# Recurrence steps that add onto Wx written ahead into PSUM, two batches at a time; a last attention tile in two halves; residual adds and stores in order of completion

## The chip, the cores and the metric

The kernel runs on one core of a Trainium2 chip. The metric is the device time of one execution in microseconds (us), the median of several runs. Engines are named as in the profile: PE is TensorE's matrix unit, DVE is VectorE, ACT is ScalarE, POOL is GpSimd, SP is the queue of SyncE that issues transfers.

## The reference

The input is x with 4 batches, 128 channels and 64 x 64 positions, so 4096 tokens a batch; all arithmetic is fp32. Layer 0 is full attention over the positions. Layer 1 works on tokens: causal attention, and then a part called ffn that ends in a recurrence over the 4096 tokens, each with a residual add.

```python
x = x + _L0_conv_ref(_gn(x), ...)           # softmax(q k) v over all positions
t = _to_tokens(x)
t = t + _L1_attn_ref(_ln_t(t), Wq, Wk, Wv)  # causal
t = t + _L1_ffn_ref(_ln_t(t), W, V, gamma, beta)

def _L1_ffn_ref(x, W, V, gamma, beta):
    Wx = x @ W.T                            # then batch norm over all 4 x 4096 tokens
    Wx = (Wx - mean) * rsqrt(var + eps) * gamma + beta
    def step(yt, wx_t):
        yt = sigmoid(wx_t + yt @ V.T)
        return (yt, yt)                     # scanned over the 4096 tokens from y = 0
```

The batch norm needs the statistics of Wx over every token of every batch, so no recurrence step can start before the last attention tile of the last batch is through.

## The kernel before

**Attention.** Batches are taken one after another, layer 0 and then layer 1. A query tile is 512 tokens (QT), eight tiles (NQ) to a batch. A tile is worked off in units of two key blocks of 128: `score` (L855) makes the scores in PSUM (L870 in layer 1, L874 in layer 0), ACT turns them into exponentials (L880, L876), DVE adds them into `total` for the softmax's denominator (L904, L908), and `product` (L889) multiplies by the values into `av` (L911). In layer 1 tile c has 2(c + 1) units, so tile 0 is the shortest and tile 7 the longest; the last four key blocks of each are triangular and are masked on POOL (L883). fp32 matmuls go through PE twice, so the profile counts two for each.

**After a tile.** `finish` (L754 to L787) turns `total` into the reciprocal of the denominator by a chain of small DVE operations (t, tt, part, side, z, rb), scales `av` into o (L775), multiplies by the value weights (po, L781) and adds the residual (L786). In layer 1, `ffn` (L730 to L752) then takes the layer norm's statistics (`deviations`, L679: PE transposes pt_f, bn_stats, POOL's power at L557), spreads them (`spread`, L694), multiplies by W (pw, L744) into w (L746), copies w into WX (ACT, L748) and takes bn_stats of it for the batch norm (L751). These pieces are generators; after each unit one piece of the tile just ended and one of the front of a list are run (`step`, L924), so their instructions stand between the units of the next tile, and PE meets them in this order.

WX of a batch is [128 channels, 32, 128]: token s * 32 + l is at [l, s]. The tokens are thus cut into 128 chunks of 32, and the recurrence runs on all chunks at once.

**Recurrence.** After the last w, DVE forms the batch norm's gain and bias (fmv, L958; fgain and fbias to L964). A chunk's true start value is not known, so 12 warm-up steps over the end of the chunk before it come first (WARM), from 0.5, and then 32 steps. Each of the 44 steps has one `advance` for each of the four batches: a matmul py = V y (L973), z = Wx * gain + py on DVE (L975), and the sigmoid with the bias on ACT (L976), which writes y over WX or, during the warm-up, over `first`:

```python
nc.tensor.matmul(ps[:, :n], lhsT=FV, rhs=y, start=True, stop=True)
nc.vector.scalar_tensor_tensor(z[:, :n], w, gain, ps[:, :n], ALU.mult, ALU.add)
nc.scalar.activation(dst, z[:, :n], AF.Sigmoid, bias=bias)
```

**End.** After each fourth step the four finished steps of every batch are added to the attention's result (L992; Y holds batches 0 to 2, X the last): 30 adds on POOL, and the last one of batches 1 and 3 on DVE. The batches are stored in the order 1, 0, 3, 2 (L996), one half issued from SP and one from ACT. A test follows of whether warm-up and true values agree (ok, good, wrong: L1002 to L1017); the engines read its result and branch, to a slower general kernel if it fails.

Of the kernel before, what the change touches and what calls it, by code (L numbers as in the profile page):

```python
# [30 lines left out]
P = 128  # L31
# [437 lines left out]
SAME = 2.0e-6  # L469


@with_exitstack
def fast_kernel(
# [78 lines left out]
    WX = {}  # L552
# [6 lines left out]
    with ExitStack() as actx:  # L559
# [13 lines left out]
        gn, K0, QR, V0, V1, Q, R1 = {}, {}, {}, {}, {}, {}, {}  # L573
# [10 lines left out]
        def merge1():  # L584
# [8 lines left out]
            wt = tmp.tile([P, 3, P], F32, tag="a", name="wt")  # L593
            center(wt, pw[:, : 3 * P].rearrange("p (a c) -> p a c", a=3), 3)
            yield
            pm = misc("pm1")
            nc.tensor.matmul(pm[:, :P], lhsT=wt[:, 0, :], rhs=wt[:, 1, :], start=True, stop=True)
# [3 lines left out]
            nc.tensor.transpose(pf[:, :P], wt[:, 2, :], ident)  # L601
# [29 lines left out]
        def keys0(b, c):  # L631

            if c == 0:
                K0[b] = kv.tile([P, N], F32R, tag="K0", name=f"K0_{b}")
                QR[b] = kv.tile([P, N // 2], F32, tag="QR", name=f"QR_{b}")
                V0[b] = wxpool.tile([P, NB, C], F32, tag="V0", name=f"V0_{b}")
# [42 lines left out]
        def deviations(src, eps, name):  # L679

            pt = misc(f"pt_{name}")
            for j in range(4):
                nc.tensor.transpose(pt[:, ts(j, P)], src[:, ts(j, P)], ident)  # L683
            stats = small.tile([P, 4, 6], F32, tag="lst", name=f"lst_{name}")
            mv = small.tile([P, 4, 2], F32, tag="lmv", name=f"lmv_{name}")
            for j in range(4):
                nc.vector.bn_stats(stats[:, j, :], pt[:, ts(j, P)])  # L687
            for j in range(4):
                nc.vector.bn_aggr(mv[:, j, :], stats[:, j, :])
            rstd = small.tile([P, 4], F32, tag="rstd", name=f"rstd_{name}")  # L690
            rsqrt(rstd, mv[:, :, 1], eps, 4)
            return pt, mv, rstd

        def spread(r, name):  # L694

            g = small.tile([P, 4, 4], F32, tag="g", name=f"g_{name}")
            for q in range(4):
                nc.vector.tensor_copy(g[0:32, :, q], r[ds(32 * q, 32), :])
            for q in range(1, 4):
                nc.vector.tensor_copy(g[ds(32 * q, 32), :, :], g[0:32, :, :])  # L700
            rb = tmp.tile([P, QT], F32, tag="r", name=f"rb_{name}", bufs=2)
            nc.vector.transpose(
                rb.rearrange("p (k j) -> p k j", j=32),
                g.rearrange("p j q -> p (j q)").unsqueeze(2).to_broadcast([P, 16, 32]),
# [25 lines left out]
        def ffn(b, c):  # L730
            if c == 0:
                last = b == B - 1
                WX[b] = wxpool.tile(
                    [P, CHUNK, NC], F32, tag="V0" if last else f"WX{b}", name=f"WX_{b}"
                )
            src = X2[b][:, ts(c, QT)]
            if b < len(kept):
                nc.sync.dma_start(out=kept[b][:, ts(c, QT)], in_=src)
            yield
            _, _, rstd = deviations(src, 1e-5, f"f_{b}_{c}")  # L740
            yield
            rb = spread(rstd, f"f_{b}_{c}")
            pw = misc(f"pw_{b}_{c}")
            nc.tensor.matmul(pw, lhsT=FWc, rhs=src, start=True, stop=True)  # L744
            w = tmp.tile([P, QT], F32, tag="w", name=f"w_{b}_{c}")
            nc.vector.tensor_tensor(w, pw, rb, ALU.mult)  # L746
            n = QT // CHUNK
            nc.scalar.copy(  # L748
                WX[b][:, :, ts(c, n)].rearrange("p l s -> p s l"), w.rearrange("p (s l) -> p s l", l=CHUNK)
            )  # L750
            nc.vector.bn_stats(stats_f[:, b * NQ + c, :], w)  # L751
            yield  # L752

        def finish(b, layer, c, av, total):  # L754

            name = f"{layer}_{b}_{c}"
            t = tmp.tile([P, QT], F32, tag="a", name=f"t_{name}")
            nc.vector.tensor_tensor(t, total[:, 0, :], total[:, 1, :], ALU.add)  # L758
            tt = tmp.tile([P, QT], F32, tag="b", name=f"tt_{name}")
            nc.vector.transpose(tt, t)  # L760
            part = small.tile([P, 16], F32, tag="part", name=f"part_{name}")
            nc.vector.tensor_reduce(part, tt.rearrange("p (k j) -> p k j", j=32), AX.X, ALU.add)
            yield
            side = small.tile([32, 4, 16], F32, tag="side", name=f"side_{name}")
            for q in range(4):
                nc.vector.tensor_copy(side[:, q, :], part[ds(32 * q, 32), :])
            z = small.tile([P, 16], F32, tag="z", name=f"z_{name}")
            nc.vector.tensor_reduce(z[0:32, :], side.rearrange("j q k -> j k q"), AX.X, ALU.add)
            nc.vector.reciprocal(z[0:32, :], z[0:32, :])
            for q in range(1, 4):  # L770
                nc.vector.tensor_copy(z[ds(32 * q, 32), :], z[0:32, :])
            rb = tmp.tile([P, 16, 32], F32, tag="a", name=f"rb_{name}")
            nc.vector.transpose(rb, z.unsqueeze(2).to_broadcast([P, 16, 32]))  # L773
            o = tmp.tile([P, QT], F32, tag="b", name=f"o_{name}")
            nc.vector.scalar_tensor_tensor(  # L775
                o, rb.rearrange("p k j -> p (k j)"), GUARD, av, ALU.mult, ALU.mult
# [3 lines left out]
            po = misc(f"po_{name}")  # L780
            nc.tensor.matmul(po, lhsT=W1v if layer else W0v, rhs=o, start=True, stop=True)  # L781
            xt = X[b][:, ts(c, QT)]
            if layer and c == 0:
                X2[b] = xpool.tile([P, N], F32, tag="X2", name=f"X2_{b}")
            dst = X2[b][:, ts(c, QT)] if layer else xt
# [4 lines left out]
        units = []  # L790
        for b in range(B):
            for layer in range(2):
                for c in range(NQ):
                    n = 2 * (c + 1) if layer else NP
                    units += [(b, layer, c, u, n) for u in range(n)]
# [11 lines left out]
        def done(key):  # L807
            if key in todo:
                todo.remove(key)
            if key in ends:  # L810
                ends.remove(key)
                _, b, layer, c = key
                if layer == 0:
                    put(("p1", b, c), prepare1(b, c))
                else:
                    put(("f", b, c), ffn(b, c))

        def begin_tile(b, layer, c):

            if layer == 0:  # L820
# [6 lines left out]
                if c == 3 and 0 < b < B - 1:  # L827
                    for k in range(NQ):
                        whole(("f", b - 1, k))
# [8 lines left out]
            else:  # L838
# [5 lines left out]
                if c + 1 < NQ:  # L844
                    todo.insert(0, ("q1", b, c + 1))
                    made["q1", b, c + 1] = after(b, c + 1)

        def after(b, c):
            whole(("e", b, 0, c))
            whole(("p1", b, c))  # L850
# [4 lines left out]
        def score(i):  # L855
            b, layer, c, u, n = units[i]
            if u == 0:
                begin_tile(b, layer, c)
# [208 lines left out]
```

## Time and profile before

| | us |
|---|---|
| median of 3 runs (2596.47 to 2599.96) | 2597.79 |
| the profiled execution | 2599.04 |
| its span in the profile | 2596.9 |
| last exponentials of the attention start (L880) | 2482.61 |
| last w (L746) starts | 2498.78 |
| table load for the sigmoid (L976), 1.28 long | 2502.93 |
| first sigmoid starts | 2504.23 |
| first store issued (L996) | 2571.12 |

The span is what the profile's page covers, from the first to the last event on the core; the execution's own time is 2.1 us longer. A busy share is an average over the span. The clock row gives the clock that PE was granted, in tenths of full speed, in 40 slices. In the chain of waits each line is a start, a length, an engine and a group of instructions, from what ended last back to what released it; in the timeline, a bracket gives the idle time ahead of an instruction and who ended it.

### The profile page before, as it was taken

How to read it: one execution, taken by the hardware profiler on the slowest of the kernel's cores; microseconds unless marked ns; L12 is line 12 of the kernel's file. 1: busy time of each engine (PE TensorE's matmuls, PEld its weight loads, DVE VectorE, ACT ScalarE, POOL GpSimd, SP SyncE). 2: the span in 40 equal slices, each digit the busy share in tenths (PEclk: the TensorE clock that was granted, in tenths of full speed). 3: DMA queues.
4: the chain of work that ended last, by engine and by line, in shares of the span. 5: the costliest groups of instructions: out<-in, count | busy, mean ns of one | idle time of the engine just before them, and what ended most of it. 6: DMA issues, size and time to landing. Idle time of an engine off the chain costs nothing.

```text
span 2596.9 us, 22102 instructions
## 1 busy us (share of the span) xinstructions
PE 2524.0 (97%) x7480; PEld 1358.2 (52%) x7480; DVE 1781.3 (69%) x3631; ACT 1153.5 (44%) x1458; POOL 231.1 (9%) x304
## 2 busy tenths in 40 slices
PE   7999999999999999999999999999999999999975
PEld 4555554444555555444555555444455555544454
DVE  7776667567867667666876666756776766776566
ACT  4444434444444444444444443444444444344455
POOL 2010001111000100110000010111100000000016
PEclk9999999999999999999999999999999999999987
DMA  2000000000100000000100000000010000000013
GB/s 72 1 0 1 0 1 13 9 4 4 37 0 1 0 1 5 12 7 6 37 0 1 1 0 1 12 9 5 5 37 0 1 1 1 0 1 1 0 65 131
DMA packets 11945, 31.31 MB, mean 12 GB/s; under 512 B 2096, under 2 KB 2864, under 8 KB 10032
## 3 DMA queue, kind: packets, MB, share of 16 engines
q1 hardware_dynamic: 8928, 24.12, 2.6%
q10 hardware_dynamic: 2896, 5.71, 0.6%
q8 instruction: 60, 0.98, 0.2%
q14 instruction: 61, 0.50, 0.1%
HBM read 15.14 MB, written 14.68 MB: 11 GB/s over the span
## 4 chain that ended last, share of the span: by engine, by line
PE 90%; DVE 6%; issue 2%; POOL 1%; ACT 1%; DMA 0%; SPq 0%; POOLq 0%; ACTq 0%; DVEq 0%
PE av L911 48%; PE ps L874 17%; PE ps L870 17%; PE py L973 2%; PE po L781 2%; DVE total L904 1%; PE pq L724 1%; PE pk L645 1%; PE pw L744 1%; POOL rstd_f L557 1%; PE pt L683 1%; DVE lst_f L687 0%; PE pt L661 0%; PE pt_f L683 0%; DVE w L746 0%
## 5 line engine op out<-in xcount | busy, mean ns | idle before, releaser
L911 PE MATMUL av<-s,V 128*128 128x512 f32 (+3 forms) x3200 | 1465.9, 580 | 5.1 <-ACT s L876 4.5
L904 DVE TENSOR_TENSOR total<-total,s 128x1024 f32<-128x1024 f32 x676 | 824.5, 1220 | 510.3 <-ACT s L876 309.6
L876 ACT ACTIVATE s<-ps,shift 128x1024 f32<-128x1024 f32 x512 | 569.1, 1114 | 772.7 <-PE ps L874 742.5
L911 PEld LDWEIGHTS av<-s,V 128*128 128x128 f32 x3200 | 594.7, 189 | 543.6 <-issue 477.0
L874 PE MATMUL ps<-q,K 128*128 128x512 f32 x2048 | 759.6, 493 | 2.0 <-DVE K L656 1.4
L880 ACT ACTIVATE s<-ps,zero,R 128x512 f32<-128x512 f32 (+1 forms) x576 | 395.8, 738 | 458.4 <-PE ps L870 457.7
L874 PEld LDWEIGHTS ps<-q,K 128*128 128x128 f32 x2048 | 386.7, 189 | 290.7 <-issue 236.2
L870 PE MATMUL ps<-q,X 128*128 128x512 f32 (+3 forms) x1152 | 500.5, 557 | 0.0
L870 PEld LDWEIGHTS ps<-q,X 128*128 128x128 f32 x1152 | 217.0, 190 | 244.4 <-issue 234.4
L557 POOL TENSOR_TENSOR rstd<-rstd,mhalf 128x4 f32<-128x4 f32 x32 | 32.7, 1023 | 1015.5 <-DVE rstd L556 1015.5
L883 POOL TENSOR_SCALAR_AFFINE_SELECT s<-s 128x128 f32<-128x128 f32 x128 | 46.6, 368 | 506.3 <-ACT s L880 505.8
L908 DVE TENSOR_TENSOR total<-total,s 128x256 f32<-128x256 f32 (+1 forms) x120 | 56.3, 493 | 43.0 <-POOL s L883 42.9
L642 POOL TENSOR_SCALAR X<-X,B0v 128x512 f32<-128x512 f32 x32 | 59.6, 1865 | 243.8 <-DVE xg L640 238.1
L786 DVE SCALAR_TENSOR_TENSOR X<-po,X 128x512 f32<-128x512 f32 x64 | 44.0, 687 | 52.5 <-PE po L781 52.0
L748 ACT COPY WX<-w 128x512 f32<-128x512 f32 x32 | 35.2, 1100 | 96.5 <-DVE w L746 96.5
L557 POOL TENSOR_TENSOR rstd_f<-rstd_f,mhalf 128x4 f32<-128x4 f32 x32 | 35.4, 1108 | 412.2 <-DVE rstd_f L556 412.2
L715 DVE TENSOR_SCALAR V<-pt,lmv,rstd 128x128 f32<-128x128 f32 x128 | 43.8, 405 | 35.8 <-POOL rstd L557 35.8
L975 DVE SCALAR_TENSOR_TENSOR z<-WX,fgain,py 128x128 f32<-128x128 f32 (+1 forms) x176 | 56.4, 347 | 6.2 <-PE py L973 1.8
L675 DVE TENSOR_TENSOR q<-QR,qh 64x512 fp32r<-64x512 f32 x64 | 43.9, 685 | 6.3 <-PE ps L874 5.6
L758 DVE TENSOR_TENSOR t<-total 128x512 f32<-128x512 f32 x64 | 44.3, 692 | 4.5 <-PE pfw L601 2.5
L775 DVE SCALAR_TENSOR_TENSOR o<-rb,av 128x512 f32<-128x512 f32 x64 | 43.8, 684 | 4.4 <-DVE rb L773 0.5
L760 DVE STREAM_TRANSPOSE tt<-t 128x512 f32<-128x512 f32 x64 | 45.4, 709 | 1.8
(120 smaller groups left out, 1328.3 us busy)
## 6 DMA issues: line engine op xcount, KB each, us to landing
X<-in_x SPq DMA_DIRECT2D x28, 256.0 KB, 5.6
kept<-X SPq DMA_DIRECT2D x24, 256.0 KB, 2.0
Y<-kept SPq DMA_DIRECT2D x6, 1024.0 KB, 7.4
out<-Y SPq DMA_DIRECT2D x3, 1024.0 KB, 8.8
out<-Y ACTq DMA_DIRECT2D x3, 1024.0 KB, 9.3
X<-in_x ACTq DMA_DIRECT2D x4, 256.0 KB, 5.7
out<-X SPq DMA_DIRECT2D x1, 1024.0 KB, 14.0
out<-X ACTq DMA_DIRECT2D x1, 1024.0 KB, 14.7
```

Source lines behind the costliest of these rows:

```text
L557: nc.gpsimd.tensor_tensor(dst, dst, mhalf[:, :n], ALU.pow)
L642: nc.gpsimd.tensor_scalar(xt, xt, B0v, None, ALU.add)
L781: nc.tensor.matmul(po, lhsT=W1v if layer else W0v, rhs=o, start=True, stop=True)
L870: nc.tensor.matmul(ps[:, h, first[h] :], lhsT=lhsT, rhs=q[:, first[h] :], start=True, stop=True)
L874: nc.tensor.matmul(ps[:, h, :], lhsT=lhsT, rhs=q[:, k, :], start=k == 0, stop=k == 1)
L876: nc.scalar.activation(s, ps, AF.Exp, bias=shift)
L880: nc.scalar.activation(part, ps[:, h, first[h] :], AF.Exp, scale=scale, bias=zero)
L904: nc.vector.tensor_tensor(total, total, s, ALU.add)
L908: nc.vector.tensor_tensor(t, t, s[:, h, first[h] :], ALU.add)
L911: nc.tensor.matmul(av[:, first[h] :], lhsT=V[:, 2 * u + h, :], rhs=s[:, h, first[h] :], start=u == 0 and h == 0, stop=u == n - 1 and h == 1,)
L973: nc.tensor.matmul(ps[:, :n], lhsT=FV, rhs=y, start=True, stop=True)
L975: nc.vector.scalar_tensor_tensor(z[:, :n], w, gain, ps[:, :n], ALU.mult, ALU.add)
```

## The change

- WX of the batches is held in pairs (WXp), and V0, layer 0's values, is a view of the last one, which the pool's tags gave before.
- In the recurrence the batches go in pairs g = 0 and 1. `seed` writes Wx * gain for four steps of a pair into two banks of PSUM on DVE; two such blocks of each pair are in flight, which takes all eight banks. `advance` adds V y onto it by a matmul without a start flag, and ACT takes the sigmoid from PSUM. Before the first two blocks of each pair, matmuls with zeros (`nil`) are made over the banks. The first block is seeded step by step.
- In layer 1 of the last batch the tiles go 0, 1, 2, 4, 5, 6, 7, 3 (LAST = 3), and the last one in two halves of 256 queries, with 7 and 8 units. `finish`, `ffn`, `deviations` and `spread` take an offset and a width.
- The last product is followed by a sigmoid of one element, so that the table is loaded there.
- POOL adds batches 0, 1 and 2, without batch 2's last two blocks; after the last step DVE adds these, and the whole of batch 3 in two halves. The stores go in the order 0, 1, 2, 3.

```diff
-    WX = {}
+
+    WXp = [wxpool.tile([P, 2, CHUNK, NC], F32, name=f"WX{g}") for g in range(B // 2)]
+    WX = [WXp[b // 2][:, b % 2] for b in range(B)]
...
-                V0[b] = wxpool.tile([P, NB, C], F32, tag="V0", name=f"V0_{b}")
+                V0[b] = WX[B - 1].rearrange("p l s -> p (l s)").rearrange("p (n c) -> p n c", c=C)
...
-        def ffn(b, c):
-            if c == 0:
-                last = b == B - 1
-                WX[b] = wxpool.tile(
-                    [P, CHUNK, NC], F32, tag="V0" if last else f"WX{b}", name=f"WX_{b}"
-                )
-            src = X2[b][:, ts(c, QT)]
+        def ffn(b, c, off, w):
+            name = f"f_{b}_{c}_{off}"
+            cols = ds(c * QT + off, w)
+            src = X2[b][:, cols]
             if b < len(kept):
-                nc.sync.dma_start(out=kept[b][:, ts(c, QT)], in_=src)
-            yield
-            _, _, rstd = deviations(src, 1e-5, f"f_{b}_{c}")
-            yield
-            rb = spread(rstd, f"f_{b}_{c}")
-            pw = misc(f"pw_{b}_{c}")
+                nc.sync.dma_start(out=kept[b][:, cols], in_=src)
+            yield
+            _, _, rstd = deviations(src, 1e-5, name)
+            yield
+            rb = spread(rstd, name)
...
+            if off == 0:
+                wt[b, c] = tmp.tile([P, QT], F32, tag="w", name=f"w_{name}")
+            part = wt[b, c][:, ds(off, w)]
+            nc.vector.tensor_tensor(part, pw, rb, ALU.mult)
             nc.scalar.copy(
-                WX[b][:, :, ts(c, n)].rearrange("p l s -> p s l"), w.rearrange("p (s l) -> p s l", l=CHUNK)
+                WX[b][:, :, ds((c * QT + off) // CHUNK, w // CHUNK)].rearrange("p l s -> p s l"),
+                part.rearrange("p (s l) -> p s l", l=CHUNK),
             )
-            nc.vector.bn_stats(stats_f[:, b * NQ + c, :], w)
...
+            if off + w == QT:
+                nc.vector.bn_stats(stats_f[:, b * NQ + c, :], wt.pop((b, c)))
...
+        def finish(b, layer, c, off, w, av, total):
+
+            name = f"{layer}_{b}_{c}_{off}"
+            k = w // 32
+            t = tmp.tile([P, QT], F32, tag="a", name=f"t_{name}")[:, :w]
+            nc.vector.tensor_tensor(t, total[:, 0, :w], total[:, 1, :w], ALU.add)
...
-        units = []
+
+        units, following = [], {}
         for b in range(B):
             for layer in range(2):
-                for c in range(NQ):
-                    n = 2 * (c + 1) if layer else NP
-                    units += [(b, layer, c, u, n) for u in range(n)]
+                order = list(range(NQ))
+                if (b, layer) == (B - 1, 1):
+                    order.append(order.pop(LAST))
+                following.update({(b, layer, c): d for c, d in zip(order, order[1:])})
+                for c in order:
+                    halves = [(0, QT // 2), (QT // 2, QT // 2)] if (b, layer, c) == (B - 1, 1, order[-1]) else [(0, QT)]
+                    for off, w in halves:
+                        n = (c * QT + off + w) // (2 * P) if layer else NP
+                        units += [(b, layer, c, off, w, u, n) for u in range(n)]
...
+            if i == len(units) - 1:
+
+                nc.scalar.activation(small.tile([P, 1], F32, name="sig"), s[:, 1, w - 1 : w], AF.Sigmoid)
...
-        zp = fctx.enter_context(tc.tile_pool(name="z", bufs=2))
-        ps_y = fctx.enter_context(tc.tile_pool(name="ps_y", bufs=1, space=PSUM))
+        ps_y = fctx.enter_context(tc.tile_pool(name="ps_y", bufs=2, space=PSUM))
...
+        nil = small.tile([P, QT], F32R, name="nil")
+        nc.vector.memset(nil.bitcast(F32), 0.0)
+        first = [small.tile([P, 2, NC], F32, name=f"first{g}") for g in range(B // 2)]
+        for g in range(B // 2):
+            nc.vector.memset(first[g], 0.5)
+        steps = list(range(CHUNK - WARM, CHUNK)) + list(range(CHUNK))
+        nk = len(steps) // BL
+        where = {}
+
+        def seed(g, k):
+            ps = where[g, k] = ps_y.tile([P, BL, 2, NC], F32, tag=f"y{g}", name=f"py{g}_{k}")
+            if k < 2:
+                for j in range(0, BL, 2):
+                    nc.tensor.matmul(
+                        ps[:, j : j + 2].rearrange("p j h s -> p (j h s)"), lhsT=nil[:, :P], rhs=nil,
+                        start=True, stop=True,
+                    )
+            j0, lo = steps[k * BL], int(k * BL < WARM)
+            for js in [slice(j, j + 1) for j in range(BL)] if k == 0 else [slice(0, BL)]:
+                nc.vector.tensor_scalar(
+                    ps[:, js, :, lo:].rearrange("p j h s -> p h j s"),
+                    WXp[g][:, :, j0 + js.start : j0 + js.stop, : NC - lo], gain, None, ALU.mult,
+                )
+
+        def advance(g, k, j):
+            n, lo = k * BL + j, int(k * BL < WARM)
+            dst = first[g][:, :, 1:] if lo else WXp[g][:, :, steps[n], :]
+            y = dst if lo else first[g] if n == WARM else WXp[g][:, :, steps[n] - 1, :]
+            ps = where[g, k][:, j, :, lo:]
+            nc.tensor.matmul(ps, lhsT=FV, rhs=y, start=False, stop=True, skip_group_check=True)
+            nc.scalar.activation(dst, ps, AF.Sigmoid, bias=bias)
+
+        def residual(eng, b, ls, cols=slice(0, NC)):
+            xj = X[b].rearrange("p (s l) -> p l s", l=CHUNK)[:, ls, cols]
+            eng.tensor_tensor(xj, xj, WX[b][:, ls, cols], ALU.add)
+
+        for k in range(2):
+            for g in range(B // 2):
+                seed(g, k)
+        for k in range(nk):
+            for j in range(BL):
+                for g in range(B // 2):
+                    advance(g, k, j)
+            if k == WARM // BL - 1:
+                for g in range(B // 2):
+                    nc.vector.memset(first[g][:, :, 0:1], 0.0)
+            for g in range(B // 2 if k + 2 < nk else 0):
+                seed(g, k + 2)
+            if k * BL >= WARM:
+                ls = slice(steps[k * BL], steps[k * BL] + BL)
+                for b in range(3 if k < nk - 2 else 2):
+                    residual(nc.gpsimd, b, ls)
+        residual(nc.vector, 2, slice(CHUNK - 2 * BL, CHUNK))
+        for h in range(2):
+            residual(nc.vector, 3, slice(0, CHUNK), ts(h, NC // 2))
         for b in range(B):
-            nc.vector.memset(first[b], 0.5)
-
-        def advance(b, y, w, dst, n):
-
-            ps = ps_y.tile([P, NC], F32, tag=f"y{b}", name=f"py{b}")
-            nc.tensor.matmul(ps[:, :n], lhsT=FV, rhs=y, start=True, stop=True)
-            z = zp.tile([P, NC], F32, tag=f"z{b}", name=f"z{b}")
-            nc.vector.scalar_tensor_tensor(z[:, :n], w, gain, ps[:, :n], ALU.mult, ALU.add)
-            nc.scalar.activation(dst, z[:, :n], AF.Sigmoid, bias=bias)
-
-        for j in range(CHUNK - WARM, CHUNK):
-            for b in range(B):
-                advance(b, first[b][:, 1:], WX[b][:, j, : NC - 1], first[b][:, 1:], NC - 1)
-        for b in range(B):
-            nc.vector.memset(first[b][:, 0:1], 0.0)
-        for j in range(CHUNK):
-            for b in range(B):
-                y = WX[b][:, j - 1, :] if j else first[b]
-                advance(b, y, WX[b][:, j, :], WX[b][:, j, :], NC)
-            if j % 4 == 3:
-                for b in range(B):
-                    js = slice(j - 3, j + 1)
-                    xj = X[b].rearrange("p (s l) -> p l s", l=CHUNK)[:, js, :]
-                    eng = nc.vector if j == CHUNK - 1 and b % 2 else nc.gpsimd
-                    eng.tensor_tensor(xj, xj, WX[b][:, js, :], ALU.add)
-        for b in (1, 0, 3, 2):
...
-                ok[:, b, 1:], first[b][:, 1:], WX[b][:, CHUNK - 1, : NC - 1], ALU.subtract
+                ok[:, b, 1:], first[b // 2][:, b % 2, 1:], WX[b][:, CHUNK - 1, : NC - 1], ALU.subtract
```

## The prediction

> **What bounds the kernel now.** I read the page's head first, then the chain that ended last, then the tail of that chain stage by stage in the windows and the timeline.
>
> ```profile
> span 2596.9 us, 22102 instructions
> PE 2524.0 (97%) x7480; PEld 1358.2 (52%) x7480; DVE 1781.3 (69%) x3631; ACT 1153.5 (44%) x1458; POOL 231.1 (9%) x304
> ...
> PEclk9999999999999999999999999999999999999987
> ...
> PE 90%; DVE 6%; issue 2%; POOL 1%; ACT 1%; DMA 0%; SPq 0%; POOLq 0%; ACTq 0%; DVEq 0%
> ```
>
> TensorE fills the attention, some 2480 us; of that only the last tile changes, so everything at stake lies in the last 115 us (4% of the span). The chain's end:
>
> ```profile
> 2490.18 2.07 PE po L781 x2
> ...
> 2504.68 60.01 PE py L973 x344
> 2564.98 8.57 DVE Y L992
> ```
>
> Three pieces are seen: a tail after the last attention tile, the recurrence (60.01 us; 43 steps at 1.395), and residual adds with the stores. In the recurrence the windows show PE, DVE and ACT all near full (columns: stretch, length, PE, PEld, DVE, ACT, POOL busy, clock, DMA share, GB/s):
>
> ```profile
> 2500.00:2510.00 10.00, 5.32 (x25) 5.32 (x26) 6.54 (x22) 7.00 (x16) 0.55 (x1) 0.50 0.00 1
> 2550.00:2560.00 10.00, 10.00 (x60) 8.65 (x59) 9.37 (x31) 9.72 (x31) 10.00 (x7) 1.00 0.00 0
> 2575.00:2580.00 5.00, 0.59 (x2) 0.50 (x2) 2.56 (x8) 0.00 (x0) 0.00 (x0) 0.50 1.02 418
> ```
>
> PE's 10.00 overstates it: 60 records of 0.318 us overlap. The first window shows the recurrence starting at half the clock (about 1.71 us a step until 2510.2, 1.36 after). The third shows stores that move 418 GB/s with nothing else running: the end is store-bound. POOL adds back to back from 2550 on, and a DVE add caught beside it is held until POOL is nearly done:
>
> ```profile
> L975 DVE SCALAR_TENSOR_TENSOR z<-WX,fgain,py 128x128 f32<-128x128 f32 (+1 forms) x176 | 56.4, 347 | 6.2 <-PE py L973 1.8
> ...
> 2564.98 8.57 DVE L992 TENSOR_TENSOR Y<-Y,WX 128x512 f32<-128x512 f32 x1
> 2569.59 2.98 POOL L992 TENSOR_TENSOR Y<-Y,WX 128x512 f32<-128x512 f32 x2
> 2571.12 2.79 SPq L996 DMA_DIRECT2D out<-Y  x2
> 2571.55 0.40 ACT L976 ACTIVATE WX<-z,fbias 128x128 f32<-128x128 f32 x1 [6.50 <-POOL Y L992]
> ```
>
> The last line: the final sigmoid sits behind a store in ACT's queue that waits for POOL.
>
> **What the Trainium skill says.** "PSUM — Partial Sum Buffer", The four PSUM rules: only TensorE sets the bits that tell a matmul without a start flag to add rather than overwrite, so a value written by VectorE is added to only where a matmul has set them before. No run here shows it; it is why eight nil matmuls exist. "GPSIMD Engine Reference", Specifications: POOL shares its SBUF interfaces with VectorE, with contention for operations with two SBUF inputs. The trace agrees: the two-input DVE add took 8.57 us against 1.11 for its like at 2573.99, while z, with one SBUF and one PSUM input, stayed at 0.347 beside a full POOL. "TensorE: Matmul & The Clock Gate", Part 1: the clock halves after an idle window; the trace has 0.50 after 2489.7 and again from 2499.95 to 2510.19.
>
> **The change part by part.** All against the profiled execution (2599.04 us, span 2596.9; the median of the runs is 2597.79, so differences carry over and the level is 1.25 lower).
>
> *Up to batch 3's layer 1* the instruction order per engine is unchanged: 0.
>
> *1. Recurrence.* Before, a batch's chain is ACT 0.402, hand-over 0.05, two fp32 passes 0.21 + 0.275 (spacing, then the last one's record), 0.04, z 0.346, 0.035: 1.36; four z of 0.347 are 1.388. VectorE and the chain bound it equally. Afterwards z is gone and two pairs of 256 columns run. Passes of 256 columns are spaced 0.2135 in the attention; the sigmoid on 256 from PSUM I put at 0.49 ("ScalarE: Activation LUTs", What ACT_TABLE_LOAD costs, gives 280 ns + 0.833 N with a pointer bias, so 493 by estimate; here 396 for 128 against its 387). Chain: 0.05 + (first weights 0.107, two passes 0.427, drain 0.168) + 0.04 + 0.49 = 1.28. PE needs 2 x 0.53 = 1.07 a step, ACT 2 x 0.49 = 0.98: the chain bounds it. 43 x 1.28 + 1.04 (last step of both pairs) = 56.1 against 61.1 (first sigmoid 2504.23 to the regular end 2565.35): **-5.0**. A sigmoid of 0.46 or 0.53 moves this by 43 x 0.035 = 1.5 either way.
>
> The seeds: 128x1024 into PSUM, two per four steps. A DVE pass of 1024 elements takes 1.22 (L904), so 2.44 in a block of 5.12: hidden in DVE, which has nothing else, and each is written a whole block ahead: it waits for the last sigmoid of the block that used its banks and is due one block later. POOL has 3 adds x 1.53 = 4.6 per 5.12: no backlog.
>
> *2. Last tile in two halves.* PE columns stay the same, but half 0's po, transposes and pw now stand before the last score: 0.43 + 0.22 + 0.43 = +1.08. Half 0's po also waits for its o, and here two normalisations meet. From half 0's last score block DVE has, in the built order: t 0.42, tt 0.44, tile 7's four bn_stats 0.95 and aggregates 0.36, part 0.40, rstd 0.17, half 1's copy 0.42, tile 7's g 1.20, rb_f 0.71, w 0.69 and statistics 0.69, side, z and reciprocal 1.65, two totals of half 1 1.38, rb 0.44, o 0.42: 10.3 (256-wide ones scaled from their 512 rows), near 11 with gaps and POOL's rstd between. PE has ten groups of four 256-column passes (pw among them) at 0.85 and 1.1 of smaller ones in that time, 9.6 in all; o reaches PE with the hand-over about 1 to 2 late. Short tiles of batches 0 to 2 show such a hole at 2.1 to 2.3 us (655.3, 1272.0, 1888.8). I take 2.3, bounds 1.5 and 3.5. A clock dip followed one such hole in three, 3.4 us at half speed, 1.7 lost: I take none, bound 1.7. Sum **+3.4** until the last score.
>
> *3. From the last exp to the first sigmoid*, 21.62 us before (2482.61 to 2504.23). Seven DVE passes of 512 become 256 (0.69 to 0.42): -1.9; po cold 2.07 to about 1.0; two bn_stats fewer -0.4; against it half 0's late ffn pieces between them on DVE, +1.3 to 2.2. To the last w: -1.5. Then 8 nil matmuls of 512 stand on PE before the first recurrence matmul, after the last reader of PSUM: 6.8 cold (8 x 0.853), 3.4 warm; the previous stage ends at clock 0.50, so mixed, 6.0, plus 0.75 to the first sigmoid, where before 4.75 passed from w, of which 1.28 was the table load that now hides. 6.75 - 4.75 = +2.0. Together **+0.5** (bounds -2.1, +1.3). The gain chain (fmv 1.03, POOL's pow 0.55) and the short first seeds lie beside the nils. The recurrence then starts warm, which the 5.0 above includes.
>
> *4. End*, R being the end of the last sigmoid. POOL ends batch 0 at R + 1.0 and batch 1 at R + 2.5 (1.53 each); DVE, two inputs, is held until then, then two ok 0.5, batch 2's 1024 elements 2.1 and batch 3's 2 x 4.0 (1.11 for 512 strided, scaled): R + 13.1. Stores start at R + 1.0; 8.39 MB took 23.7 us from first issue to last landing, so R + 24.7 if they don't run dry, and they don't: a batch takes 5 us at 418 GB/s, so batch 2, ready at R + 5, and batch 3 at R + 13 come before the queue is empty at R + 18. Flag: 3.7 us more of DVE and PE to R + 16.8, load and branch 1.5, restart of the engines 7.2 (2579.8 to 2587.0 before), R + 25.5. Final wait to end took 2.0: R + 27 to 27.6 against 31.55 (2565.35 to 2596.9): **-3.95** (bounds -4.5, -1).
>
> Sum: -5.0 + 3.4 + 0.5 - 3.95 = **-5.05**: span 2591.9, and from the median 2597.79 **2592.7 us**. Likeliest case's own range: 2590 to 2596.
>
> **Rivals.**
> A. The half tile gives back the rest: hole 3.5, dip 1.7, nils cold. +1.2 + 1.7 + 0.8: -1.35, **2596.4**. For it: DVE was 0.74 busy already from 2482 to 2492, and gets more. Against: the clock held at two of three such holes.
> B. Slower: the seeds, like the 8.57 us add, are held while POOL adds back to back. Seeds and adds are released by the same sigmoid; held for 4.6, they end 7.0 after the block, where the next but one is due at 5.1: 1.9 lost in each of the six blocks that have both, +11.4: **2604.1**. It decides once a hold exceeds 5.12 - 2.44 = 2.7 us. Against: a seed has one SBUF input, as z has, and z wasn't held.
> C. More gain: hole 1.5 (-0.8), nils nearly warm (-2.5), sigmoid 0.47 (-0.9): -9.25, **2588.5**. For it: PE was fast again between 2496.5 and 2499.95.
> That the sums go wrong through unset bits and the flag sends the work to the general kernel would cost far more; every seeded bank had a nil matmul over its whole width first, so 0.01, inside slower.
>
> **How the numbers follow.** Forecast 0.45, A 0.17, B 0.13, C 0.25. A measurement of this kernel tells 0.2% (5.2 us, 2592.6) from nothing; the forecast lies on that edge: 0.25 faster, 0.20 same. C is faster; A 0.14 same, 0.03 slower with both bounds at the end added; B slower. Faster 0.50, same 0.34, slower 0.16. The range takes in A, C and their bounds, not B: 2585 to 2600.
>
> **What would show it.** Recurrence: sigmoids of one pair 1.28 apart, 43 of them; at 1.36 or more step 1 is wrong. Seeds at 1.2 us: over 3, B. Part 2: the last score 3.4 later, one hole before half 0's po. Part 3: eight nils between the last w and the first sigmoid, 6 us. Part 4: first store 1 us after the last sigmoid, the last landing some 24 later. A landing that waits for DVE's batch 3, or a branch after R + 19, makes the end wrong.

## The result, and the profile after

The changed kernel takes 2594.39 us in the median of 22 runs (2592.44 to 2596.96), the kernel before 2598.97 in as many (2596.24 to 2600.01). The ratio is 0.9985 with an interval of 0.9979 to 0.9992: a gain of about 4 us, clear of the scatter, but smaller than the 0.2% that the prediction took as the least to be told from nothing. The profiled execution has a span of 2592.4 us against 2596.9.

The page of the changed kernel, its head; and from its chain that ended last, the end:

```profile
span 2592.4 us, 21739 instructions
PE 2519.8 (97%) x7372; PEld 1345.1 (52%) x7372; DVE 1760.3 (68%) x3513; ACT 1139.7 (44%) x1386; POOL 219.7 (8%) x297
```

```profile
2506.19 2.33 DVE py L1010 x6
2509.88 3.73 PE py L1020 x8
2566.97 3.34 DVE Y L1025
2570.31 7.68 DVE X L1025 x2
```

Where 60.01 us of PE stood there are only 3.73 in one piece: the chain now changes engine at every step, from matmul to sigmoid and back, so the view leaves the short pieces out. New are the first seeds (L1010) ahead of the recurrence, and DVE's adds behind it.

The timeline of the changed kernel (start, length, engine, line; in brackets the idle time ahead and who ended it) shows the three places that decide, and at its end the verdict of the test:

```profile
2479.69 1.22 PE L788 MATMUL po<-o,W1v 128*128 128x256 f32 x2 [2.58 <-DVE o L782]
...
2502.82 3.75 PE L1004 MATMUL py<-nil 128*128 128x512 f32 x8 [3.35 <-DVE w_f L751]
2503.43 1.02 DVE L981 BATCH_NORM_AGGREGATE fmv<-fstats 128x2 f32<-128x192 f32 x1
...
2506.11 5.14 DVE L1010 TENSOR_SCALAR py<-WX,fgain 128x254 f32<-128x254 f32 x9
...
2508.57 1.12 PE L1020 MATMUL py<-first,FV 128*128 128x254 f32 x4 [2.00 <-DVE py L1010]
2509.36 0.84 ACT L1021 ACTIVATE first<-py,fbias 128x254 f32<-128x254 f32 x2 [6.02 <-PE py L1020]
...
2566.86 3.81 SPq L1049 DMA_DIRECT2D out<-Y  x3
...
2581.33 0.14 DVE L1070 CAST wrong<-good 1x1 int32<-1x1 f32 x1
```

First, PE idles 2.58 us for half 0's o. Second, the matrices of zeros are through at 2506.57, and PE then idles another 2.00 for seeds. Third, the first store goes 1.0 after the last sigmoid ends (2565.87). The windows of the changed kernel (stretch, length, busy time of PE, PEld, DVE, ACT and POOL, clock, DMA share, GB/s) add the clock after the hole, the stores at the end, and what is busy in the middle of the recurrence:

```profile
2479.00:2483.00 4.00, 3.31 (x8) 2.71 (x9) 2.22 (x5) 0.66 (x2) 0.00 (x0) 0.57 0.01 2
...
2575.00:2580.00 5.00, 0.00 (x0) 0.00 (x0) 4.90 (x6) 0.00 (x0) 0.00 (x0) 0.50 1.01 418
```

```profile
2525.00:2545.00 20.00, 18.60 (x65) 9.30 (x64) 9.68 (x9) 15.14 (x32) 14.06 (x10) 1.00 0.01 1
```

The clock fell to half right at the hole. The stores still move 418 GB/s. In the recurrence ACT and DVE stand idle a quarter and half of the time, and PE's 18.60 counts each matmul to its modelled end, while its weight loads are busy 9.30. The timeline of one step:

```profile
2560.87 0.30 PEld L1020 LDWEIGHTS py<-WX,FV 128*128 128x128 f32 x2 [0.49 <-ACT WX L1021]
2561.35 0.30 PEld L1020 LDWEIGHTS py<-WX,FV 128*128 128x128 f32 x2 [0.18 <-ACT WX L1021]
2561.61 0.96 ACT L1021 ACTIVATE WX<-py,fbias 128x256 f32<-128x256 f32 x2 [0.31 <-PE py L1020]
```

In each step of 1.26 PE's weight loads wait 0.67 for ACT, and ACT waits 0.31 for PE. So no engine is full, and a step is bound by one pair's chain.

All kernels below are read by the same five stages, from starts in their timelines: A from the first exponentials of batch 3's layer 1 to the last pair of them; B from there to the last w; C to the first sigmoid; D to the end of the last sigmoid; E to the end of the span.

| kernel | A | B | C | D | E | span |
|---|---|---|---|---|---|---|
| before | 247.20 | 16.17 | 5.44 | 61.12 | 31.55 | 2596.9 |
| changed | 252.75 | 15.37 | 7.11 | 56.51 | 26.53 | 2592.4 |
| e1, tile 7 whole | 247.20 | 17.34 | 7.90 | 55.98 | 26.6 | 2590.2 |
| e9, tile 7 in halves | 251.34 | 13.16 | 7.11 | 56.51 | 26.3 | 2588.3 |
| e2, po later | 249.95 | 15.51 | 7.63 | 55.97 | 26.4 | 2589.1 |
| e3, seeds by bank | 251.26 | 15.36 | 5.11 | 55.29 | 26.4 | 2588.7 |
| e4, no batch 3 add | 252.37 | 15.36 | 7.17 | 56.13 | 21.6 | 2586.8 |
| e8, early batch 3 | 251.27 | 15.36 | 7.63 | 62.92 | 26.4 | 2597.5 |
| e5, end as before | 251.27 | 15.36 | 7.63 | 56.63 | 34.1 | 2601.3 |
| e6, single batches | 251.26 | 15.37 | 5.07 | 47.20 | 28.5 | 2582.9 |
| e7, pairs with z | 251.27 | 15.32 | 4.03 | 80.08 | 26.4 | 2611.8 |
| c2 | 251.27 | 15.36 | 5.07 | 47.08 | 26.9 | 2581.3 |
| c1 | 251.36 | 13.17 | 4.77 | 47.19 | 26.8 | 2578.8 |

(The last sigmoid of before counts at its regular end, 2565.35. e4, e5, e6 and e7 were run once each, the others four times or more.) Three things are to be known for this table.

- Stage A of one and the same code is 251.26 or 251.27 in the six profiles without a clock drop in it (e3, e5, e6, e7, e8, c2), and 252.75 in the changed kernel's, which has one. e4's, 252.37, has a drop too, but is no seventh of these: in its trace tile 7's ffn pieces stand 1.7 us earlier in PE's order.
- The start of stage A, after 2234 us in which PE and ACT do the same instructions in all kernels, scatters from 2233.7 to 2236.4. So 1.3 us of the 4.5 between the two spans (2235.42 before, 2234.12 changed) lie within this scatter and can't be counted for the change.
- Stage C with the changed kernel's seeds is 7.1 where the clock was back at full for the first matmul (changed, e9, e4), and 7.6 where it was still at half with the same last tile (e2, e5, e8).

### The profile page after: what moved, and what is told of

Read it like the earlier page. It is cut to its first block, busy times and chain, and to the rows that moved or that the text cites. A ratio compares the mean times of both kernels' runs of the same rounds, so it can differ in the third digit from the quotient of the medians.

```text
span 2592.4 us, 21739 instructions
## 1 busy us (share of the span) xinstructions
PE 2519.8 (97%) x7372; PEld 1345.1 (52%) x7372; DVE 1760.3 (68%) x3513; ACT 1139.7 (44%) x1386; POOL 219.7 (8%) x297
## 4 chain that ended last, share of the span: by engine, by line
PE 89%; DVE 6%; issue 2%; ACT 1%; POOL 1%; DMA 0%; SPq 0%; POOLq 0%; ACTq 0%; DVEq 0%
PE av L932 48%; PE ps L895 17%; PE ps L888 17%; PE po L788 2%; DVE total L929 1%; PE py L1020 1%; PE pq L730 1%; PE pk L649 1%; POOL rstd_f L561 1%; PE pw_f L747 1%; ACT WX L1021 1%; PE pt L688 1%; DVE lst_f L692 0%; PE pt L665 0%; DVE w_f L751 0%
## 5 line engine op out<-in xcount | busy, mean ns | idle before, releaser
L929 DVE TENSOR_TENSOR total<-total,s 128x1024 f32<-128x1024 f32 (+4 forms) x802 | 881.6, 1103 | 553.4 <-ACT s L897 308.9
L932 PE MATMUL av<-s,WX 128*128 128x512 f32 x2048 | 964.4, 593 | 3.4 <-ACT s L897 3.4
L932 PEld LDWEIGHTS av<-s,WX 128*128 128x128 f32 x2048 | 382.2, 189 | 312.0 <-issue 270.0
L932 PE MATMUL av<-s,V 128*128 128x512 f32 (+3 forms) x1180 | 504.7, 549 | 0.6 <-ACT s L901 0.6
L932 PEld LDWEIGHTS av<-s,V 128*128 128x128 f32 x1180 | 218.8, 191 | 226.1 <-issue 201.6
L794 DVE SCALAR_TENSOR_TENSOR X<-po,X 128x512 f32<-128x512 f32 (+1 forms) x65 | 44.1, 678 | 51.3 <-PE po L788 50.9
L752 ACT COPY WX<-w_f 128x512 f32<-128x512 f32 (+1 forms) x33 | 35.3, 1069 | 93.1 <-DVE w_f L751 93.1
L561 POOL TENSOR_TENSOR rstd_f<-rstd_f,mhalf 128x4 f32<-128x4 f32 (+1 forms) x33 | 36.1, 1094 | 398.6 <-DVE rstd_f L560 398.6
L765 DVE TENSOR_TENSOR t<-total 128x512 f32<-128x512 f32 (+1 forms) x65 | 44.5, 684 | 4.5 <-PE pfw L605 2.5
L782 DVE SCALAR_TENSOR_TENSOR o<-rb,av 128x512 f32<-128x512 f32 (+1 forms) x65 | 43.9, 675 | 4.4 <-DVE rb L780 0.5
```

Of the source, the lines that this page charges most:

```text
L561: nc.gpsimd.tensor_tensor(dst, dst, mhalf[:, :n], ALU.pow)
L765: nc.vector.tensor_tensor(t, total[:, 0, :w], total[:, 1, :w], ALU.add)
L794: nc.vector.scalar_tensor_tensor(dst, po, 1.0 / GUARD, xt, ALU.mult, ALU.add)
L929: nc.vector.tensor_tensor(t, t, s[:, h, f:w], ALU.add)
L932: nc.tensor.matmul(av[:, first[h] : w], lhsT=V[:, 2 * u + h, :], rhs=s[:, h, first[h] : w], start=u == 0 and h == 0, stop=u == n - 1 and h ...
```

## The experiments

### Part 2: the halves

e1 puts the order of the tiles and the last tile back; e9 keeps the halves but cuts tile 7; e2 lets half 0's po stand one unit later.

```diff
# e1 (the first two) and e9 (the first alone)
-LAST = 3
+LAST = 7
-                    halves = [(0, QT // 2), (QT // 2, QT // 2)] if (b, layer, c) == (B - 1, 1, order[-1]) else [(0, QT)]
+                    halves = [(0, QT)]
# e2
+            if w < QT:
+                yield
             po = misc(f"po_{name}")[:, :w]
```

> Tile order of before (tile 7 last) and the last tile whole: part 2 of the change undone, all else as changed. Theory (the halves of tile 3 cost more than they bring): last exponentials start near 2482.6 us as before instead of 2486.9, last w starts 16.2 later (15.4 in the changed kernel), first sigmoid 6.9 after that, so near 2505.9 against 2509.4; recurrence and end as changed; span about 2589, some 3.5 below the changed kernel, 0.997 of before. Rival (the halves pay by the shorter tail, and the matrices of zeros run cold without them): first sigmoid at 2509 or later, span 2592 or more.

> Tile 7 last, in two halves of 15 and 16 units. Theory (the hole at half 0's po comes from tile 7's ffn work meeting half 0's normaliser on DVE, because tile 3 has too few units): with tile 6's ffn done long before, DVE has 5.5 us to do where PE has 9.6, so no hole above 0.5 us and no dip of the clock there; last exponentials near 2483.7, half 0's ffn done before them, last w 13 us later, first sigmoid near 2503.8, span about 2587, 5 below the changed kernel, 0.996 of before. Rival (the hole belongs to halving as such: o follows its half's end too closely): a hole of 2 us or more before half 0's po, last exponentials at 2486 or later, span 2590 or more.

> As changed, with half-width po put one unit later in PE's order. Theory (hole and dip are lost at this place only): hole before half 0's po under 1 us, clock 1.0 in the four us after 2479, last exponentials near 2483.8, about 3 earlier; half 0's ffn ends a unit later, so last w 16 us after them; span about 2590. Rival (DVE is the bound of the whole stretch): the hole returns at a later instruction, last exponentials at 2486 or later, span unchanged at 2592.

Measured: e1 0.9975 of before (0.9964 to 0.9985), first sigmoid at 2507.60; e9 0.9975 (0.9964 to 0.9985), 2505.50; e2 0.9976 (0.9966 to 0.9986), 2506.77. The intervals overlap with that of the change, so the totals alone don't settle it; the stages do. From the start of stage A to the last w, the whole tile 7 takes 247.20 + 17.34 = 264.54, tile 7 in halves 251.34 + 13.16 = 264.50, tile 3 in halves 266.6, with the clock drop 268.1. So cutting tile 7 moves 4 us from behind the last exponentials to ahead of them and gains nothing by itself; with tile 3 it loses 2.1, with the drop 3.6. e1's expectation held in direction, not in size: its tail was 1.2 longer than before's and its stage C a microsecond longer than expected. It gained 2.2 in the span in place of 3.5; its stages are 3.2 shorter in sum, since its stage A began 1.05 later than that of the changed kernel.

The holes, in the timelines of e9 and of e2 (with ACT's copy ahead of it):

```profile
2449.92 0.70 PE L932 MATMUL av<-s,V 128*128 128x256 f32 x2 [1.40 <-ACT s L901]
```

```profile
2476.43 1.06 ACT L752 COPY WX<-w_f 128x512 f32<-128x512 f32 x1 [2.17 <-DVE w_f L751]
...
2477.90 1.15 PE L934 MATMUL av<-s,V 128*128 128x256 f32 x4 [1.24 <-ACT s L903]
...
2479.75 0.59 PE L790 MATMUL po<-o,W1v 128*128 128x256 f32 x2
```

In e9 no wait for o is left, as expected, but a new one of 1.40 stands in the midst of half 0: the theory was right about its hole and missed this one, and the last exponentials came at 2485.2 and not 2483.7. In e2 po starts without a wait and the clock stays at 1.00; a hole of 1.24 is left, for exponentials.

Both holes that are left have one origin, which neither theory had. The copy of the last whole tile's w into WX, on ACT, waits for DVE's w_f and takes 1.06; the next exponentials stand behind it in ACT's queue, and PE's products wait for them. In e9 the copy starts at 2448.46 and the exponentials at 2449.32, in e2 at 2476.43 and 2477.30. In the changed kernel they are as late, at 2476.88 and 2477.75, but there the wait for o covers it.

e2's stage A is 2.8 shorter than that of the profiled changed kernel, near the theory's 3, but 1.5 of this is the clock drop, which six profiles of the same code lack. Against those the edit is worth 1.3. So the theory was right about what it named, and the rival in that a hole came back, though at an earlier instruction than po.

### Part 3: what the first matmul waits for

```diff
-            ps = where[g, k] = ps_y.tile([P, BL, 2, NC], F32, tag=f"y{g}", name=f"py{g}_{k}")
+            ps = where[g, m] = ps_y.tile([P, 2, 2, NC], F32, tag=f"y{g}", name=f"py{g}_{m}")
...
-            for js in [slice(j, j + 1) for j in range(BL)] if k == 0 else [slice(0, BL)]:
-                nc.vector.tensor_scalar(
+            nc.vector.tensor_scalar(
+                ps[:, :, :, lo:].rearrange("p j h s -> p h j s"),
+                WXp[g][:, :, j0 : j0 + 2, : NC - lo], gain, None, ALU.mult,
...
```

> Seeds of two steps, each pair's block in a bank of its own (four in flight), in place of four steps in two banks with the first block step by step. Theory (the first advance waits for all seven single-step seeds ahead of it, 2.7 us, and not for the matrices of zeros): first matmul of the recurrence near 0.8 after the gain is ready and at the end of the zeros, 2506.6 in place of 2508.6; last w to first sigmoid 5.1 in place of 7.1; step unchanged at 1.27; span about 2590.4. Rival (twice the seeds at 0.74 each disturb DVE and the chain, or the zeros are what is waited for): first matmul at 2508 or later, or a step of 1.3 and more, no gain.

Measured: 0.9972 of before (0.9961 to 0.9983). The timeline of e3:

```profile
2502.49 3.75 PE L1003 MATMUL py<-nil 128*128 128x512 f32 x8 [3.34 <-DVE w_f L751]
...
2505.31 0.74 DVE L1007 TENSOR_SCALAR py<-WX,fgain 128x508 f32<-128x508 f32 x1
...
2506.11 6.23 PE L1017 MATMUL py<-first,FV 128*128 128x254 f32 x19
2507.03 1.00 ACT L1018 ACTIVATE first<-py,fbias 128x254 f32<-128x254 f32 x2 [4.02 <-PE py L1017]
```

The recurrence's first matmul starts 0.06 after the first seed's end and follows the zeros with no wait; stage C is 2.0 shorter, as the theory had it. A second gain came with it that was not expected: PE is no longer idle before the recurrence, its clock doesn't drop in the first steps, and stage D is 1.2 shorter. The step itself is unchanged (1.26).

### Part 1: pairs, and z

```diff
# e6: each batch by itself
...
-            ps = where[g, k][:, j, :, lo:]
+            ps = where[b, k][:, j, lo:]
             nc.tensor.matmul(ps, lhsT=FV, rhs=y, start=False, stop=True, skip_group_check=True)
             nc.scalar.activation(dst, ps, AF.Sigmoid, bias=bias)
...
# e7: pairs, z on DVE, no seeds
...
+            nc.tensor.matmul(ps[:, :, lo:], lhsT=FV, rhs=y, start=True, stop=True)
+            nc.vector.scalar_tensor_tensor(
+                z[:, :, lo:], WXp[g][:, :, steps[n], : NC - lo], gain, ps[:, :, lo:], ALU.mult, ALU.add
+            )
+            nc.scalar.activation(dst, z[:, :, lo:], AF.Sigmoid, bias=bias)
...
```

> As changed, with each batch by itself: 176 matmuls and sigmoids on 128 columns, adding onto seeds of 512 elements. Theory (without z the chain of a batch is only 0.98, but then ACT is the bound: four sigmoids of 128 in a step, 0.35 to 0.39 each, and PE's four pairs of passes 1.3): a step of 1.40 to 1.55, recurrence of 61 to 67 us against 56.5. Rival (taking z out was all of it, pairs are no matter): a step of 1.3 or less.

> As changed, in pairs of 256 columns, but with z on DVE as before, no seeds and no matrices of zeros: the fourth of the four cases {pair, single} x {z, seed}, of which the steps so far are single with z 1.36, pair with seed 1.27, single with seed 1.06. Theory (a step is the longer of one group's chain and the busiest engine; a pair makes the chain longer by about 0.3): chain 1.27 + 0.07 + 0.42 to 0.48 = 1.76 to 1.82 in a step, recurrence of 77 to 80 us. Rival (the chain is hidden by the other pair, and only engine time counts: PE 1.07, ACT 0.95, DVE 0.96): a step of 1.3 or less, recurrence of 57 or less.

e6 was the surprise: 2584.96 us in its one run, stage D 47.2. Against the theory, single batches are faster than pairs, by 9.3 in stage D, or by 8.1 against e3, which has no clock drop there. The step fell in the rival's range, but not because pairs are no matter. The windows of e6 in the same stretch as above, and two groups of instructions (busy time and mean ns of one, idle time before):

```profile
2525.00:2545.00 20.00, 20.00 (x157) 20.00 (x156) 13.25 (x20) 20.00 (x79) 20.00 (x14) 1.00 0.01 1
...
L1016 ACT ACTIVATE WX<-py,fbias 128x128 f32<-128x128 f32 x128 | 33.3, 448 | 0.0
L1015 PEld LDWEIGHTS py<-WX,FV 128*128 128x128 f32 x248 | 32.1, 188 | 0.0
```

PE, its weight loads, ACT and POOL all read as full, but records overlap, so the window alone doesn't tell which of them bounds. ACT does. 128 sigmoids in 33.3 us are one every 0.26, four to a step of 1.03; their records are 0.36 long in the first steps and grow to 0.45 once they stand back to back. The first weight load of a batch starts 0.05 after a sigmoid ends, the second 0.11 later, and the next comes 0.15 after that, with the next sigmoid's end: PE waits for ACT. Eight loads 0.11 apart would take 0.9 (an estimate from these gaps). The theory took the record of a sigmoid in the kernel before, 0.35 to 0.39, for the time that ACT needs for it.

e7 came as the theory had it, with a step of 1.81 and 80.1 us; two steps of its timeline:

```profile
2540.69 1.13 ACT L1007 ACTIVATE WX<-z,fbias 128x256 f32<-128x256 f32 x2 [0.68 <-DVE z L1004]
...
2542.50 1.14 ACT L1007 ACTIVATE WX<-z,fbias 128x256 f32<-128x256 f32 x2 [0.68 <-DVE z L1004]
```

Together, the step by its two factors (the median from one sigmoid of a batch or pair to its next):

| | z on DVE | adding onto seeds |
|---|---|---|
| single batches | 1.36 (before) | 1.03 (e6) |
| pairs | 1.81 (e7) | 1.26 (changed) |

Taking z out is worth 0.33 to 0.55 a step; pairing costs 0.23 to 0.45. In a pair each matmul and sigmoid of the chain is longer, and two chains don't fill an engine (ACT is idle a quarter of the time); with four the bound is ACT's own work, which is shorter than the pair's chain.

### Part 4: the end

```diff
# e4: batch 3's residual left out
-        for h in range(2):
-            residual(nc.vector, 3, slice(0, CHUNK), ts(h, NC // 2))
# e8: the same adds cut by time step
-        for h in range(2):
-            residual(nc.vector, 3, slice(0, CHUNK), ts(h, NC // 2))
+        for q in range(4):
+            for h in range(2):
+                residual(nc.vector, 3, ts(q, CHUNK // 4), ts(h, NC // 2))
# e5: adds and stores as before
-                for b in range(3 if k < nk - 2 else 2):
-                    residual(nc.gpsimd, b, ls)
...
+                for b in range(B):
+                    residual(nc.vector if k == nk - 1 and b % 2 else nc.gpsimd, b, ls)
+        for b in (1, 0, 3, 2):
```

> As changed, but the residual of batch 3 is not added (8 us of DVE after the last sigmoid left out; its output holds the attention's result alone). R is the end of the last sigmoid; in the changed kernel the verdict is written at R + 15.6, PE's branch takes 7.7 us, and the span ends at R + 26.5. Theory (the branch after the verdict sets the end, and the stores are through 2 to 3 us sooner): verdict near R + 7.5, the end then set by the last landing, R + 22 to 24. Rival (the stores set the end, as the prediction had it): R + 26 or more.

> As changed, with batch 3's adds on DVE cut into eight of 512 elements by time step, six of which stand between the seeds of the last blocks, while POOL is adding. Theory A (a two-input add on DVE beside POOL's adds is held, with the seeds queued behind it): these adds take 3 to 5 us each in place of 1.1, seeds end late, and single steps of the recurrence grow from 1.27 to 2 and more: the last sigmoid 2 to 8 us later, and what the end gains (verdict 6 us earlier, end near R + 24) is lost: span 2592 or more. Theory B (held adds find gaps, seeds have a block's lead): the recurrence stays at 56.5 and the end comes at R + 24, span near 2590.

> As changed, with the residual adds and the order of the stores as before (30 adds on POOL, two on DVE, batches stored 1, 0, 3, 2). Theory (the order of completion is worth what the prediction gave it, about 4, and more now that a block is shorter): 4 adds of 1.56 fill 6.2 of each block of 5.07, POOL ends 9 us after the last sigmoid, the first store goes at R + 6 to 8, the end is at R + 32 or later against R + 26.5. Rival (the stores were never behind POOL): end at R + 28 or less.

e4 ended at R + 21.6, which looks like the theory, but it tells less than it should: with no add to wait for, batch 3's two stores left at 2465.0 and 2497.6 already, so a quarter of the stores was gone as well. e8 decides instead: its verdict was written at R + 10.0 (R the end of the last sigmoid), 5.6 us earlier than in the changed kernel, and PE's branch ended at R + 19.3. The last store still landed at R + 24.6, and the end came at R + 26.4, where both of e8's theories had R + 24. So an earlier verdict gains nothing here; the stores set the end, though the chain of waits names DVE's adds. In the changed kernel both are through at once: PE's branch ends at 2590.52, SP's wait for the stores at 2590.59.

e8's own theory A held for the adds and the recurrence. Its DVE timeline:

```profile
2546.34 10.96 DVE L1025 TENSOR_TENSOR X<-X,WX 128x512 f32<-128x512 f32 x2
2557.16 4.82 DVE L1010 TENSOR_SCALAR py<-WX,fgain 128x1024 f32<-128x1024 f32 x4
...
2580.94 0.14 DVE L1071 CAST wrong<-good 1x1 int32<-1x1 f32 x1
```

Two adds of 512 elements took 10.96 us beside POOL's adds, the seeds stood behind them, and stage D grew by 6.4: 1.0001 of before (0.9992 to 1.001), with runs from 2593.47 to 2601.75.

e5 lost 7.5 in stage E, in one run of 2603.41. Its first store went 8.9 after the last sigmoid, later than the 6 to 8 expected, and one DVE add stood beside POOL's for most of that time:

```profile
2566.76 11.90 DVE L1025 TENSOR_TENSOR Y<-Y,WX 128x512 f32<-128x512 f32 x1 [7.64 <-ACT WX L1021]
```

The order of completion is worth more here than the 5.0 by which stage E fell with the change. A likely reason is that POOL has less time per block to keep up with all four batches; e5 puts the adds and the order of the stores back together, so their shares are not shown.

### The two that beat both

c2 is e6 with batch 2's last three blocks, in place of two, added by DVE; c1 has tile 7 in halves as well.

```diff
# c1 alone
-LAST = 3
+LAST = 7
# c1 and c2
-                for b in range(3 if k < nk - 2 else 2):
+                for b in range(3 if k < nk - 3 else 2):
-        residual(nc.vector, 2, slice(CHUNK - 2 * BL, CHUNK))
+        residual(nc.vector, 2, slice(CHUNK - 3 * BL, CHUNK))
```

> Tile 7 last in two halves, each batch by itself in the recurrence, and batch 2's last three blocks (in place of two) added by DVE, so that POOL is not behind. Theory (the gains add): last exponentials near 2485.2, last w 13.2 later, first sigmoid 5.1 after that, 2503.5; recurrence 47.2; first store 1.0 after the last sigmoid and the end 26.5 after it: span 2577, ratio to before 0.992 to 0.993. Rival (POOL and DVE hold each other up once a block takes only 4.25): first store 3 after the last sigmoid and a recurrence of 48 or more, span 2580 or more.

> As the kernel with each batch by itself, tile 3 last in two halves as changed, with batch 2's last three blocks added by DVE. Theory: first sigmoid near 2507.2, recurrence 47.2, end 26.5 after the last sigmoid: span near 2581, some 11 below the changed kernel, ratio to before 0.994. Rival: the first store stays 3 after the last sigmoid, span 2583 as with two blocks.

c1: 2580.79 us, 0.9926 of before (0.9912 to 0.9939). c2: 2583.45 us, 0.994 (0.9924 to 0.9955). Stages B to D came as expected in both, but for c1's C, which was 0.3 shorter; the first store goes 1.4 and 1.6 after the last sigmoid, down from 3.0 in e6 and short of the 1.0 expected. c1's span of 2578.8 against 2577 is mostly a late start of its stage A (2235.56, e9's 2233.89). In these two it is the branch that ends last: with a block more for DVE to add, the verdict comes at R + 17.3 and R + 17.6 and PE's branch ends at R + 25.8 and R + 25.9, while the last store lands at R + 23.7 and R + 23.9. An earlier verdict, which gained nothing in e8, could gain here; no run shows it.

## Why the prediction was right

The time lies in its range, 1.7 above its 2592.7 (the kernel before came out 1.2 above the runs it started from), and the sign was right. It had held a gain of more than 0.2% likeliest, at 0.50; what came is its second case, less than 0.2%, at 0.34. Its sum of -5.05 met -4.5 in the profiles, in part by luck: 1.3 of the 4.5 lie in the start of stage A, and terms that were off cancelled. The stages A to E are 3.2 shorter in these two executions. That holds a clock drop of 1.5 which six profiles of the same code lack; without it the stages would be 4.7 shorter, and the medians differ by 4.6.

**Step 1, the recurrence: -5.0 forecast, -4.6 measured.** The step was 1.26 for 1.28, the sigmoid 0.474 for 0.49, and the chain bounds it, as stated. What failed is the clause that the recurrence "then starts warm": PE idled 2.0 us before it, the clock fell again at 2510.0 for 3.4 us, and 1.2 us went there: that is what stage D of e3 has less, without the idle time. The seeds took 1.28 beside POOL's adds for 1.22: rival B is out for one-input writes. Its mechanism is real for two-input adds, as e8 shows. The prediction asked whether the chain or an engine bounds the pair, and never what the chain would be without the pair; that is where most of what was left lay.

**Step 2, the halves: +3.4 forecast, +4.07 without the clock drop, +5.55 in the profile.** The hole was 2.58 for 2.3, and the wait is the one forecast, for o. What the prediction did not have is the second wait under it, for exponentials behind ACT's copy, which e2 shows. The drop that was taken as none did fall there in this profile, at 1.5; of seven profiles of the same code one has it. Rival A's part of the story was thus real in the profiled execution, though not in the other six.

**Step 3: to the end of the last w -1.1 for -1.5, from there +1.9 for +2.0.** (The prediction counts to the end of w, the table to its start, where it is -0.8 and +1.7.) The second was right by luck, for the wrong reason. The eight zeros took 3.75 us, not 6.0: they are of type fp32r and start 0.43 apart at half clock, so "6.8 cold (8 x 0.853)" was twice too much; 0.853 is the spacing of an fp32 matmul's passes at half clock (pw in the kernel before). And the statement that "the short first seeds lie beside the nils" failed: the first matmul started 0.06 after the seventh of the eight single-step seeds had ended, and PE idled 2.0 us behind the zeros. In e3, where the first tile is one seed in one bank, this wait is gone. That it is the four seeds of the matmul's own tile that are waited for, with the other pair's between them, fits the times but is not shown apart.

**Step 4: -3.95 forecast, -5.0 measured.** First store at R + 1.0 and last landing at R + 24.7 were both met to a tenth. What was too long was the branch's end at R + 25.5 with 2.0 behind it: it came at R + 24.65, and 1.85 followed. DVE's adds ended at R + 12.1 for 13.1.

e1's tail is 1.2 longer than that of before, and the traces place it: from the start of t to the end of o DVE takes 6.79 in e1 and 5.62 in before. The memsets of nil and of ok, 0.48 each, now stand between these links, where before had ok's behind o. Whether moving them away gives the 1.2 back stays open, since no run did.

## What to carry to other kernels

Before two recurrences are joined to halve the instructions, write the chain of one group beside the load of each engine: joining shortens the loads and lengthens the chain. Here the pair's chain, 1.26, came out longer than the 1.03 that ACT needs for four single sigmoids. Take the load of an engine from how often it starts an instruction when it has work waiting, not from the length of a record. A test of the two factors apart, here pairs and z, costs one run each and showed that one of them was a loss. Work that was moved from behind the last score to ahead of it was paid in full here: 4.1 more ahead for 4.2 less behind (e9 against e1).

## What the hardware showed that was not expected

- A sigmoid on 128 columns has a record of 0.36 us when ACT has waited for it and of 0.45 when they stand back to back, but then four of them fit into 1.03 (e6).
- A DVE add with two inputs in SBUF is held while POOL's adds stand back to back (11.90 us for one in e5 and 8.57 in before, each ending 1.0 after the last of POOL's adds, 10.96 for two in e8, 1.11 alone); a one-input write into PSUM beside the same adds took 1.28.
- After a hole of 2.58 us on PE the clock halves in some executions and not in others: it did at half 0 in one profile of seven of the same code, for 3.4 us, and cost 1.5.
- At half clock an fp32r matmul of 512 columns started every 0.43 us (L1004), a pass of an fp32 one every 0.85 (pw in before).
- PE's branch after the verdict took 7.1 to 8.0 us in the thirteen profiles; the other engines' branches took under 0.1.
